# A fused attention, state-space and expert layer on one core: three reorderings (lone late matmuls ahead of the turns, the time step's additions between context differences, a projection over all columns)

## The chip, the cores and the metric

The kernel runs on one core of a Trainium2 chip. The metric is the device time of one execution in microseconds (us), the median of several runs. TensorE multiplies matrices and writes to PSUM, VectorE (DVE in the profile), ScalarE (ACT) and GpSimd (POOL) work on elements, SyncE (SP) issues most transfers. PEld is TensorE's loading of weights.

## What is computed

A layer of a perceiver for a batch of 16 sequences of 128 rows and 512 channels, in 32 bit floating point throughout. Cut to what matters:

```python
x = x + xattn(layernorm(x), ctx)        # 16 heads of 32; 2048 context rows a sequence
x = x + mamba_block(layernorm(x))       # below, then rmsnorm, an MLP of 2048, rmsnorm
x = x + experts(layernorm(x))           # a shared and an expert product, a gate of 7

# in mamba_block, inner width 1024, state 16:
x, z  = split(Z @ in_proj)
x     = silu(causal_conv(x))
dt, B, C = split(x @ x_proj, [32, 48])  # 32 + 16 + 16 columns
dt    = softplus(dt @ dt_proj + b)
h[t]  = exp(dt*A) * h[t-1] + dt * B * x
y     = (sum over states of h*C + x*D) * silu(z)
return y @ out_proj
```

## The kernel before

The program is written in an order set out by hand: each engine executes its instructions in the order in which the Python code issues them, and semaphores keep the data right between the engines.

The attention is cut into 256 steps, `u` = 0 to 255 (L1196): 16 sequences, 4 blocks of 512 context rows for each, 4 groups of 4 heads for each block. After these, 58 more steps and a rest finish the state-space scans and the MLP. In a step the following stands in this order:

- `scores(u)` (L297): four products of queries and keys into four PSUM banks (bank 0 to 3), and `weighted(u - 1)` (L341), the values of the step before under its weights.
- `maxima` (L307, VectorE) and `exps` (L314, ScalarE) read each bank.
- `x_products` (L274) and, at the step's end, `y_products` (L286) make the keys and values of the next block. They are a seven-product scheme for 2 x 2 blocks (the table at L189): the products take blocks of the context, or differences of them, t1 to t4, which GpSimd forms in `ctx_sums` (L221) at steps with u % 4 == 1. The first `y_products` after that need t2, the `x_products` of the next step need t3.
- `turn(u, i, bank)` (L329), i = 0 to 3: four transposes of the weights into a bank, which ScalarE copies out (VectorE for i = 2).
- In between, on VectorE, ScalarE and GpSimd, a quarter of the scan of one chunk of 128 channels: `decays` (L659, exponentials of dt), `inputs` (L637, dx times B), `scan` (L674, twice a step).

Other work is put into the steps by dictionaries of due steps (L1079 to L1136): `late` for matmuls after the turns, `behind` for those after them, `middle`, `inner`, `after`, `head` and `loads` for the rest. Those that matter here:

- `scaled(b, 0)` (L456) at u % 16 == 3: transposes of the shares `fx` into a bank, which VectorE multiplies with `avs`. `turned(b)` (L386) at u % 16 == 10: transposes of the normed x, which VectorE copies out (L391). In some steps with u % 16 == 10 other late matmuls stand beside it.
- A late matmul gets bank 3, 0, 1, ... in turn (`places`, L1257), or the bank of `avp` or `pc` in some steps. If it takes one of the four banks, only three turns are done before it, and the fourth goes behind it, into the next bank (L1263 to L1279). With a single late matmul in bank 3 the fourth turn goes into bank 0.
- `dt_first`, `dt_second`, `dt_third` (L607, L622, L629) make the time step of a chunk. `dt_third` is two additions and a product of 128 x 256 on GpSimd (L631, L632, L634): dt, which `decays` reads, and dx, which `inputs` reads. It is due in `inner`, at the end of steps with u % 4 == 0, from u = 52 on, every fourth step, 64 times.
- `x_proj(g)` (L577), once for each of 8 pairs of sequences, is a product with 64 columns of weights (32 + 16 + 16) in eight parts, each part two instructions on TensorE. Its weights lie in `xproj`, 8 x 64 columns a partition.

Of the kernel before, what the change touches and what calls it, by code (L numbers as in the profile page):

```python
# [8 lines left out]
FP = mybir.dt.float32  # L9
# [6 lines left out]
P = 128  # L16
# [4 lines left out]
DI, DS, DTR = 1024, 16, 32  # L21
EC = DI // P
# [3 lines left out]
GT = GB * NQ  # L26
# [8 lines left out]
def perceiver_layer(ctx: ExitStack, tc: tile.TileContext, a: dict, out: bass.AP):  # L35
    nc = tc.nc
# [21 lines left out]
    bcd = [dram.tile([2 * DS, GT], FP, tag=f"bcd{g}", name=f"bcd{g}") for g in range(B // GB)]  # L58
# [50 lines left out]
    with ExitStack() as es:  # L109
        acon = es.enter_context(tc.tile_pool(name="acon", bufs=1))  # L110
# [7 lines left out]
        def acon_in(name, shape, src=None):  # L118
            t = acon.tile(shape, FP, tag=name, name=name)
            nc.gpsimd.dma_start(t, a[name] if src is None else src)  # L120
            return t
# [3 lines left out]
        banks = [psum.tile([P, 512], FP, tag=f"s{j}", name=f"bank{j}") for j in range(4)]  # L125
# [95 lines left out]
        def ctx_sums(g, names):  # L221
            b11, b12, b21, b22 = (ctx_t[g, j, c] for j in range(2) for c in range(2))
            for n in names:
                t = pool.tile([P, 2, 256], FP, tag=n, name=f"{n}_{g}", bufs=1)
                cfac[g, n] = t
                x, y = {
                    "t1": lambda: (b12, b11),
                    "t2": lambda: (b22, cfac[g, "t1"]),
                    "t3": lambda: (b22, b12),
                    "t4": lambda: (b21, cfac[g, "t2"]),  # L230
                }[n]()
                nc.gpsimd.tensor_tensor(t, x, y, ALU.subtract)  # L232
# [247 lines left out]
            moments_of(b)  # L480


        xproj = acon_in("xproj", [P, EC, DTR + 2 * DS])
        convw = acon_in("convw", [P, EC, 4])
        convb = acon_in("convb", [P, EC])
        dtb = acon_in("dtb", [P, EC])
# [3 lines left out]
        zTs, xas, zss, bcs, dts, wts, ysum, wts_in = ({} for _ in range(8))  # L490
# [84 lines left out]
            sgs.clear()  # L575

        def x_proj(g, ps):  # L577
            ps = ps[0 : DTR + 2 * DS, 0:GT]
            for ec in range(EC):
                nc.tensor.matmul(  # L580
                    ps, xproj[:, ec, :], xas[g, ec], start=(ec == 0), stop=(ec == EC - 1)
                )
            nc.vector.tensor_copy(xd[0 : DTR + 2 * DS, :], ps)
            nc.sync.dma_start(bcd[g], xd[DTR : DTR + 2 * DS, :])

        def load_bc(t, base):

# [11 lines left out]
        xd = ssm.tile([P, GT], FP, tag="xd", name="xd", bufs=1)  # L599
# [29 lines left out]
        def dt_third(g, ec):  # L629
            dt, e, u = dts[g, ec]  # L630
            nc.gpsimd.tensor_tensor(dt, dt, e, ALU.subtract)  # L631
            nc.gpsimd.tensor_tensor(dt, dt, u, ALU.add)  # L632
            dx = ssm.tile([P, GT], FP, tag="dx", name="dx")
            nc.gpsimd.tensor_tensor(dx, dt, xas[g, ec], ALU.mult)  # L634
            dts[g, ec] = dt, dx
# [118 lines left out]
        def flat(ps):  # L754
            return ps.rearrange("p k q -> p (k q)")
# [320 lines left out]
            )  # L1076


        late, after, inner, middle, loads, head, behind = ({} for _ in range(7))  # L1079

        def put(where, u, f):
            where.setdefault(u, []).append(f)

        for b in range(B):
            s = 16 * b
# [21 lines left out]
        for g in range(NG):  # L1107
            p = 32 * (g + 1)
            for ec in range(EC):
                put(loads, p + 8 + ec, lambda g=g, ec=ec: load_win(g, ec))  # L1110
                put(loads, p + 8 + ec, lambda g=g, ec=ec: load_win(g, EC + ec))
                put(late, p + 9 + ec, lambda ps, g=g, ec=ec: x_part(g, ec, ps))
                put(late, p + 9 + ec, lambda ps, g=g, ec=ec: z_part(g, ec, ps))
                put(after, p + 10 + ec, lambda g=g, ec=ec: silu_first(g, ec, xas))
                put(after, p + Z_GATES[ec], lambda g=g, ec=ec: silu_first(g, ec, zss))
            put(late, p + 18, lambda ps, g=g: x_proj(g, ps))
            s = p + LAG
            for ec in range(EC):
                put(loads, s - 4 + 4 * ec, lambda ec=ec: load_dtproj(ec))
                put(behind, s - 3 + 4 * ec, lambda ps, g=g, ec=ec: dt_first(g, ec, ps))  # L1120
                put(middle, s - 2 + 4 * ec, lambda g=g, ec=ec: dt_second(g, ec))
                put(inner, s - 2 + 4 * ec, lambda g=g, ec=ec: dt_third(g, ec))
            for i in range(GB):
                for ec in range(WS):
                    put(loads, s + 32 + 2 * i, lambda g=g, i=i, ec=ec: load_wout(g, i, ec))
                put(loads, s + 31 + 2 * i, lambda b=g * GB + i: reload_x(b))
                put(late, s + 33 + 2 * i, lambda ps, g=g, i=i: projected(g, i, ps))
# [68 lines left out]
        for u in range(last):  # L1196
            live = u < NU
            g, r = divmod(u - 32 - LAG, 32)
            scans = 0 <= g < NG

            made, phase = divmod(u + 3, 4)
            makes = 0 < made < B * SB
            of, phase = ("k", "v")[phase // 2], phase % 2
            load_bc(u + 2 - 32 - LAG, 0)
            if u % 4 == 1 and made + 1 < B * SB:
                load_ctx(made + 1, ("c00", "c10", "c11"))
            if u % 4 == 2 and made + 1 < B * SB:
                load_ctx(made + 1, ("c01",))
            for f in loads.get(u, ()):
                f()  # L1210
            if scans:
                decays(g, r, 0)
            if u > NU:
                while fed < feeds * (u - NU) // (last - 1 - NU):
                    feed(fed)
                    fed += 1
            load_bc(u + 1 - 32 - LAG, DS)
            if u == NU + 1:
                load_rows()
            if live:  # L1220
                scores(u)
            if 1 <= u <= NU:
                weighted(u - 1)
            if u == NU:
                att.close()
                give_back(flat(pa), banks[2], banks[1], flat(avp))
                open_ffn()
            if u == NU + 8:
                load_wex()
            for f in head.get(u, ()):  # L1230
                f()
            if live:
                maxima(u)
            if makes:
                x_products(of, made, phase, pa, pc)
            if live:
                exps(u)
            if makes and u % 4 == 1:
                ctx_sums(made, ("t1", "t2"))
            if 0 <= u + 1 - 32 - LAG < 32 * NG:  # L1240
                inputs(*divmod(u + 1 - 32 - LAG, 32))
            if makes and u % 4 == 1:
                ctx_sums(made, ("t3", "t4"))
            silu_third()
            if scans:
                scan(g, r, 0)
            if makes:
                hold(of, made, pa, "u1")
            if scans:
                decays(g, r, 1)  # L1250
            if makes:
                x_sums(of, made, phase, pa, pc)

            after_turns = late.get(u, ())
            places = [banks[(3 + i) % 4] for i in range(len(after_turns))]  # L1257
            if live and after_turns:
                if u % 4 == 0:
                    places = [flat(avp), *places[:-1]]  # L1260
                elif u % 2 and makes and u not in behind:
                    places[-1] = flat(pc)
            taken = sum(any(p is b for b in banks) for p in places)  # L1263
            if live:
                for i in range(3 if taken else 4):
                    turn(u, i, i)
            if scans:
                scan(g, r, 1)
            for f in middle.get(u, ()):
                f()  # L1270
            for f, ps in zip(after_turns, places):
                if live:
                    f(ps)
                else:
                    ps = bank()
                    f(ps)
                    give_back(ps)
            if live and taken:
                turn(u, 3, (3 + taken) % 4)  # L1279
            for f in behind.get(u, ()):  # L1280
                ps = flat(pc) if makes else banks[2] if live else bank()
                f(ps)
                if not live:
                    give_back(ps)
            for f in after.get(u, ()):
                f()
            for f in inner.get(u, ()):
                f()
            if makes:
                y_products(of, made, phase, pa, pc)  # L1290
                y_sums(of, made, phase, pa, pc)
            silu_second()
# [76 lines left out]
```

## Time and profile before

| | us |
|---|---|
| median of 3 runs | 3802.73 (3801.78 to 3805.72) |
| the profiled execution's own time | 3809.03 |
| its span, first to last instruction | 3807.2 |
| TensorE busy in the span | 3747.0 |
| from 44 to 3110 us, the attention's steps: TensorE busy of 3066.0 | 3044.5 |
| from 3110 us on: TensorE busy of 697.0 | 666.6 |

The mean granted clock of TensorE is 0.993 of full speed. The steps of the attention take 9.2 us (three block products) to 18.0 us (four, with a late projection in it).

How to read it: a row of a timeline gives start, duration, engine, line of the kernel, operation, what it writes and reads (out<-in), the shape, and xN for N instructions run together; in square brackets the idle time before it and what ended it. The ends of matmuls are modelled, and they overlap the next start, so times between starts are the surer measure on TensorE.

### The profile page before, as it was taken

How to read it: one execution, taken by the hardware profiler on the slowest of the kernel's cores; microseconds unless marked ns; L12 is line 12 of the kernel's file. 1: busy time of each engine (PE TensorE's matmuls, PEld its weight loads, DVE VectorE, ACT ScalarE, POOL GpSimd, SP SyncE). 2: the span in 40 equal slices, each digit the busy share in tenths (PEclk: the TensorE clock that was granted, in tenths of full speed). 3: DMA queues.
4: the chain of work that ended last, by engine and by line, in shares of the span. 5: the costliest groups of instructions: out<-in, count | busy, mean ns of one | idle time of the engine just before them, and what ended most of it. 6: DMA issues, size and time to landing. Idle time of an engine off the chain costs nothing.

```text
span 3807.2 us, 70317 instructions
## 1 busy us (share of the span) xinstructions
PE 3747.0 (98%) x26120; PEld 2858.7 (75%) x26120; DVE 2690.4 (71%) x4852; ACT 2443.9 (64%) x5847; POOL 2107.1 (55%) x1968
## 2 busy tenths in 40 slices
PE   8999999999999999999999999999999989999999
PEld 7878787778777877787778878787878766655555
DVE  3444445887878777877787778877887777767843
ACT  3555556777767776777677767776777665545421
POOL 2111213675667665766676566666676667567730
PEclk9999999999999999999999999999999989999999
DMA  3111122444444435353534353445344457577752
GB/s 101 34 40 43 55 65 79 136 154 139 137 162 141 156 120 176 129 166 118 175 131 156 116 187 128 148 134 178 131 148 136 159 186 263 191 256 257 263 194 72
DMA packets 341223, 548.40 MB, mean 144 GB/s; under 512 B 24432, under 2 KB 225408, under 8 KB 340624
## 3 DMA queue, kind: packets, MB, share of 16 engines
q1 hardware_dynamic: 340464, 543.28, 43.2%
q8 instruction: 206, 3.38, 0.4%
q14 instruction: 137, 1.12, 0.1%
q0 software_dynamic: 416, 0.63, 0.1%
HBM read 527.29 MB, written 16.52 MB: 143 GB/s over the span
## 4 chain that ended last, share of the span: by engine, by line
PE 90%; DVE 5%; ACT 3%; issue 1%; POOL 1%; DMA 1%; SPq 0%; DVEq 0%; POOLq 0%; ACTq 0%
PE pa L240 24%; PE pc L240 17%; PE bank L333 11%; PE bank L302 7%; PE avp L346 6%; PE bank L526 4%; PE bank L873 3%; PE bank L968 2%; PE bank L842 2%; PE bank L472 2%; PE avp L399 1%; PE bank L707 1%; PE pc L707 1%; PE pa L873 1%; PE pc L526 1%
## 5 line engine op out<-in xcount | busy, mean ns | idle before, releaser
L310 DVE TENSOR_REDUCE nm<-bank 128x1 f32<-128x512 f32 x1024 | 635.3, 682 | 250.2 <-PE bank L302 250.0
L694 POOL TENSOR_TENSOR ysum<-ysum,w 128x512 f32<-128x512 f32 x384 | 500.7, 1304 | 487.7 <-DVE hst L657 305.8
L320 ACT ACTIVATE pr<-bank,nm 128x512 f32<-128x512 f32 x1024 | 689.8, 687 | 101.0 <-DVE nm L310 97.0
L643 POOL TENSOR_TENSOR w<-dx,bc 128x512 f32<-128x512 f32 x512 | 653.0, 1296 | 4.7
L678 DVE TENSOR_TENSOR_SCAN hst<-hst,w 128x512 f32<-128x512 f32 x456 | 557.0, 1221 | 12.8 <-ACT hst L664 8.5
L338 ACT COPY pT<-bank 128x512 f32<-128x512 f32 x816 | 434.9, 585 | 183.2 <-PE bank L333 179.4
L333 PE MATMUL bank<-ident,pr 128*128 128x128 f32 x4096 | 517.5, 274 | 14.4 <-ACT pr L320 10.5
L664 ACT ACTIVATE hst<-dt,alog 128x254 f32<-128x254 f32 x912 | 436.5, 479 | 145.5 <-DVE hst L657 126.1
L333 PEld LDWEIGHTS bank<-ident,pr 128*128 128x128 f32 x4096 | 471.4, 142 | 66.1 <-ACT pr L320 17.0
L346 PEld LDWEIGHTS avp<-pT,v 128*32 128x32 f32 x8192 | 208.6, 110 | 195.0 <-issue 177.4
L681 DVE TENSOR_TENSOR w<-hst,bc 128x512 f32<-128x512 f32 x456 | 315.2, 691 | 21.2 <-DMA bc<-bcd 5.7
L232 POOL TENSOR_TENSOR t<-c,c 128x512 f32<-128x512 f32 x128 | 164.4, 1285 | 259.4 <-PE pc L240 253.2
L302 PE MATMUL bank<-kt,qT 32*128 32x512 f32 x2048 | 301.3, 643 | 0.9 <-ACT pT L338 0.9
L346 PE MATMUL avp<-pT,v 128*32 128x128 f32 x8192 | 277.6, 276 | 0.0
L240 PE MATMUL pa<-t,ks 128*128 128x256 f32 x1024 | 249.8, 387 | 6.1 <-POOL t L232 6.1
L240 PE MATMUL pa<-vs,t 128*128 128x256 f32 x1008 | 244.7, 386 | 0.0
L240 PEld LDWEIGHTS pa<-t,ks 128*128 128x128 f32 x1024 | 184.8, 190 | 44.2 <-issue 10.6
L240 PEld LDWEIGHTS pa<-vs,t 128*128 128x128 f32 x1008 | 185.4, 190 | 34.6 <-issue 10.1
L320 ACT ACTIVATION_READ_ACCUMULATOR pr<-bank,nm 128x1 f32 x1024 | 209.9, 205 | 0.0
L336 DVE COPY pT<-bank 128x512 f32<-128x512 f32 x208 | 143.8, 691 | 89.6 <-PE bank L333 88.1
L232 POOL TENSOR_TENSOR t<-c,t 128x512 f32<-128x512 f32 x128 | 163.4, 1276 | 36.5 <-issue 19.6
L526 PE MATMUL bank<-zT,win 128*128 128x256 f32 x792 | 182.7, 381 | 0.0
(319 smaller groups left out, 6890.4 us busy)
## 6 DMA issues: line engine op xcount, KB each, us to landing
bc<-bcd SPq DMA_DIRECT2D x512, 512.0 KB, 4.3
c<-in_ctxT_dram SPq DMA_DIRECT2D x256, 256.0 KB, 4.3
wf<-in_w_dram SPq DMA_DIRECT2D x128, 512.0 KB, 7.0
wqo<-in_wqkvo_dram SPq DMA_DIRECT2D x128, 256.0 KB, 4.9
win<-in_win_dram SPq DMA_DIRECT2D x128, 256.0 KB, 4.5
wout<-in_wout_dram SPq DMA_DIRECT2D x128, 256.0 KB, 4.0
x<-in_x_dram SPq DMA_DIRECT2D x16, 256.0 KB, 4.3
x1d<-x SPq DMA_DIRECT2D x16, 256.0 KB, 2.1
```

Of the source, the lines that this page charges most:

```text
L240: nc.tensor.matmul(ps[:, r, :], l[:, kc, r * P : (r + 1) * P], m[:, kc, :], start=(i in (1, 2, 5) and r == 0 and kc == 0), stop=(r == 1 an ...
L302: nc.tensor.matmul(banks[j], qts[b][rows, hg, :], kts[u // 4, hg][rows, :], start=True, stop=True)
L310: nc.vector.tensor_reduce(stats[b][0][j][:, sb, hg : hg + 1], banks[j], AX.X, ALU.max, negate=True)
L320: nc.scalar.activation(pr[:, j, :], banks[j], AF.Exp, bias=nm[j][:, sb, hg : hg + 1], accum_out=sm[:, sb, h : h + 1],)
L333: nc.tensor.transpose(ps[:, j, :], prs[u][:, j, i * P : (i + 1) * P], ident)
L338: nc.scalar.copy(pT, ps)
L346: nc.tensor.matmul(avp[j * HD : (j + 1) * HD, hg, :], vts[u // 4, hg // 2, i // 2][:, i % 2, hg % 2 * P + j * HD : hg % 2 * P + (j + 1) * HD],
L526: nc.tensor.matmul(ps, w[:, kc, :], zTs[g][:, kc, :], start=(kc == 0), stop=(kc == KC - 1))
L643: nc.gpsimd.tensor_tensor(w, dx.unsqueeze(1).to_broadcast([P, NH // 2, GT]), bcs[g * 32 + r, 0][:, i * NH // 2 : (i + 1) * NH // 2, :], AL ...
L664: nc.scalar.activation(bt(h[:, k, :])[:, :, 1:], bt(dt)[:, :, 1:], AF.Exp, scale=aneg[:, ec, n : n + 1],)
L678: nc.vector.tensor_tensor_scan(flat, flat, w.rearrange("p n t -> p (n t)"), 0.0, ALU.mult, ALU.add)
L694: nc.gpsimd.tensor_tensor(s, s, w, ALU.add)
```

## The change

Three edits, independent of each other.

1. `xproj` gets 64 more columns, set to zero by a memset on VectorE at the start; `x_proj` takes 128 columns of weights for each part (its own 64 and the next part's) and writes all 128 partitions of the bank. VectorE still copies the first 64 rows.
2. `dt_third` moves from the end of a step with u % 4 == 0 to the next step, between the differences t1, t2 and `inputs`; t3 and t4 follow `inputs` as before.
3. In a step with u % 16 of 3 or 10 and exactly one late matmul, this is issued ahead of the turns, into bank 3, and all four turns follow in banks 0 to 3. That is so for `scaled(b, 0)` at u = 19, 35, ..., 243 (fifteen steps) and for `turned` at u = 10, 26, 58, 90, 122, 154, 186, 218. VectorE's read of that bank is then also issued ahead of its copy of turn 2 and of the second `scan`.

```diff
-        xproj = acon_in("xproj", [P, EC, DTR + 2 * DS])
+
+        NX = DTR + 2 * DS
+        xproj = acon.tile([P, EC * NX + P - NX], FP, tag="xproj", name="xproj")
+        nc.gpsimd.dma_start(xproj[:, 0 : EC * NX], a["xproj"].rearrange("p a b -> p (a b)"))
+        nc.vector.memset(xproj[:, EC * NX :], 0.0)
...
         def x_proj(g, ps):
-            ps = ps[0 : DTR + 2 * DS, 0:GT]
+            ps = ps[:, 0:GT]
             for ec in range(EC):
                 nc.tensor.matmul(
-                    ps, xproj[:, ec, :], xas[g, ec], start=(ec == 0), stop=(ec == EC - 1)
-                )
-            nc.vector.tensor_copy(xd[0 : DTR + 2 * DS, :], ps)
-            nc.sync.dma_start(bcd[g], xd[DTR : DTR + 2 * DS, :])
+                    ps,
+                    xproj[:, ec * NX : ec * NX + P],
+                    xas[g, ec],
+                    start=(ec == 0),
+                    stop=(ec == EC - 1),
+                )
+            nc.vector.tensor_copy(xd[0:NX, :], ps[0:NX, :])
+            nc.sync.dma_start(bcd[g], xd[DTR:NX, :])
...
-                put(inner, s - 2 + 4 * ec, lambda g=g, ec=ec: dt_third(g, ec))
+                put(between, s - 1 + 4 * ec, lambda g=g, ec=ec: dt_third(g, ec))
...
             if makes and u % 4 == 1:
                 ctx_sums(made, ("t1", "t2"))
+            for f in between.get(u, ()):
+                f()
             if 0 <= u + 1 - 32 - LAG < 32 * NG:
                 inputs(*divmod(u + 1 - 32 - LAG, 32))
...
+
+            ahead = live and u % 16 in (3, 10) and len(after_turns) == 1
+            if ahead:
+                after_turns[0](banks[3])
+                after_turns, places = (), ()
             taken = sum(any(p is b for b in banks) for p in places)
```

More of the change, by code (lines that the diff above doesn't have):

```diff
@@ L1076, in perceiver_layer @@
             )
-        late, after, inner, middle, loads, head, behind = ({} for _ in range(7))
+        late, after, inner, middle, loads, head, behind, between = ({} for _ in range(8))
         def put(where, u, f):
```

## The prediction

> **What bounds the kernel now.** I read the page first, then who waits for whom on TensorE, then the timelines of TensorE, GpSimd and VectorE in the steps that the change touches.
>
> ```profile
> PE 3747.0 (98%) x26120; PEld 2858.7 (75%) x26120; DVE 2690.4 (71%) x4852; ACT 2443.9 (64%) x5847; POOL 2107.1 (55%) x1968
> PE 90%; DVE 5%; ACT 3%; issue 1%; POOL 1%; DMA 1%; SPq 0%; DVEq 0%; POOLq 0%; ACTq 0%
> ```
>
> TensorE is busy 98% of the span and is 90% of the chain that ended last. A gain can only come from TensorE having less to do or waiting less. Its waits:
>
> ```profile
> PE pa L240 <- POOL t L232: 6.1, 12, 0.5
> ...
> PE bank L333 <- ACT pT L338: 3.3, 6, 1.3
> ```
>
> The columns are total us, times, longest. Twelve waits for a context difference and six for a copy out of a bank: these two rows are what the change can reach. "Idle" there counts from modelled ends of matmuls, so I work below with starts. In an undisturbed stream a transpose starts 0.109 us after the one before, a 256-column product 0.216 us.
>
> **Part 1: the time step's additions behind the first two differences.** At u % 16 == 5, from u = 69 to 245, twelve times, TensorE looks like this (u = 165):
>
> ```profile
> 1993.98 1.91 PE L333 MATMUL bank<-ident,pr 128*128 128x128 f32 x16
> 1996.39 1.99 PE L240 MATMUL pa<-t,ks 128*128 128x256 f32 x8 [0.50 <-POOL t L232]
> ...
> 2000.40 1.99 PE L240 MATMUL pa<-t,ks 128*128 128x256 f32 x8
> ```
>
> Sixteen transposes from 1993.98 end their issue at 1993.98 + 16 x 0.109 = 1995.72; the next product starts at 1996.39, so 0.67 us is lost. It needs t2. GpSimd in that stretch:
>
> ```profile
> 1985.94 1.46 POOL L694 TENSOR_TENSOR ysum<-ysum,w 128x512 f32<-128x512 f32 x1 [3.37 <-DVE hst L657]
> 1987.35 4.11 POOL L467 TENSOR_TENSOR aT<-aT,avs 128x512 f32<-128x512 f32 x3
> 1991.42 0.72 POOL L631 TENSOR_TENSOR dt<-dt,e 128x256 f32<-128x256 f32 x1
> 1992.22 0.72 POOL L632 TENSOR_TENSOR dt<-dt,l 128x256 f32<-128x256 f32 x1
> 1993.02 0.73 POOL L634 TENSOR_TENSOR dx<-dt,xa 128x256 f32<-128x256 f32 x1
> 1993.71 1.27 POOL L232 TENSOR_TENSOR t<-c,c 128x512 f32<-128x512 f32 x1
> 1995.06 1.28 POOL L232 TENSOR_TENSOR t<-c,t 128x512 f32<-128x512 f32 x1
> 1996.29 2.50 POOL L643 TENSOR_TENSOR w<-dx,bc 128x512 f32<-128x512 f32 x2
> 1998.74 1.28 POOL L232 TENSOR_TENSOR t<-c,c 128x512 f32<-128x512 f32 x1
> ```
>
> From 1985.94 GpSimd never rests. The change puts the three additions (2.33 us) behind t1 and t2. These then end at 1991.42 + 1.27 + 0.08 + 1.27 = 1994.04, which is 1.7 us before TensorE asks. The wait of 0.67 us goes.
>
> What is late next is t3, the last row shown. The order after is t1, t2, dt, dt, dx, w, w, t3: the same work, started from the same release by VectorE, which hangs on the step before and does not move. So t3 ends no earlier than now, 2000.02. It ends slightly later: the rows show 0.08 us between an operation and one that reads its result, against an overlap of 0.04 otherwise. Now one such gap (t1 to t2) and two (L631, L632, L634) are there; after, w follows dx at once and reads it, a gap in place of an overlap: 0.12 us more, t3 at 2000.14. Add 0.055 us from t2's end (1996.34) to its product (1996.39): TensorE can start on t3 at 2000.20. It starts now at 2000.40 and would arrive at 2000.40 - 0.67 = 1999.73. So 0.47 us of the 0.67 comes back as a wait for t3 in the next step, and 0.20 remains: 12 x 0.20 = 2.4 us. In the other steps with these additions t2 is ready 1.8 us or more before its product, and t3 2.1 us or more, so nothing is gained or lost there.
>
> What the move delays: dt by two differences, 2.55 us. Its first reader is the exponential at L664 on ScalarE. In the attention's steps that starts at least 5.9 us after dt is done (1992.94 and 1998.90 here), so 2.7 us are left once TensorE comes 0.67 us earlier: no cost. Behind the attention there are no differences, and the additions stay directly ahead of w, except twice, where two additions of b2 (L883, 2.5 us) now go first. In the first of these ScalarE already waits 2.0 us for dt and would wait 2.5 longer (3468.10 to 3470.6); in the other about 1.1 (3540.69 to 3541.8). VectorE uses these decays only at 3475.53 and 3548.79, and ScalarE's next operations lie at 3473.82 and 3547.07: hidden. Without that cover it would be 3.6 us in all, which I keep for the range.
>
> **Part 2: a lone late matmul ahead of the turns.** Two kinds. At u % 16 == 10, where `turned` is alone (u = 10, 26, 58, 90, 122, 154, 186, 218), TensorE at u = 154 shows:
>
> ```profile
> 1874.21 1.47 PE L333 MATMUL bank<-ident,pr 128*128 128x128 f32 x12
> 1875.52 0.60 PE L389 MATMUL bank<-ident,xn 128*128 128x128 f32 x4
> 1876.53 0.66 PE L333 MATMUL bank<-ident,pr 128*128 128x128 f32 x4 [0.41 <-ACT pT L338]
> ```
>
> The fourth turn uses bank 0 and waits for ScalarE's copy of the first: 1876.53 - (1875.52 + 4 x 0.109) = 0.57 us. After, `turned` starts at 1874.21, the turns at 1874.65, and the fourth turn, on bank 3, is due at 1874.65 + 12 x 0.109 = 1875.96. It must wait for VectorE's copy of bank 3 (L391), now issued ahead of the second scan, right behind these sums:
>
> ```profile
> 1874.48 0.88 DVE L260 SCALAR_TENSOR_TENSOR kt<-pc,bk,u1k 128x256 f32<-128x256 f32 x2
> ```
>
> They end at 1875.36; the copy starts 0.08 us before that end, as neighbours in this row do, takes 0.69, and 0.06 us later the turn may start: 1876.03. A wait of 0.07 takes the place of 0.57: 0.50 us gained, five times (u = 90 to 218), 2.5 us. At u = 58 ScalarE's exponentials are late; `turned` on bank 3 must then sit out the last of them, and the sums end at 695.01, so the fourth turn starts at 695.67 in place of 696.19: 0.5 us. At u = 10 and 26 there is no wait now, and the new one costs 0.07 each. Sum: 2.5 + 0.5 - 0.1 = 2.9 us.
>
> At u % 16 == 3 `scaled` is alone (u = 19 to 243, fifteen times), and no wait is seen there now. After, VectorE's product (L464, 0.68) follows one sum (L270, 1971.54 to 1972.23 at u = 163): 1972.23 - 0.08 + 0.68 + 0.06 = 1972.89, and the fourth turn is due at 1971.27 + 0.44 + 1.31 = 1973.02. Nothing gained, 0.12 us short of a loss. Behind the matmul on TensorE all four turns are queued, but its inputs are there over 3 us earlier and bank 3 is free when the last exponential ends, which the first turn needs too. The read-out passes VectorE's copy of turn 2 and a scan; these come up to 0.7 us later, and VectorE idled 0.41 us before the next maxima here.
>
> **Part 3: x_proj over 128 columns.** The row first (u = 50):
>
> ```profile
> 601.15 1.47 PE L333 MATMUL bank<-ident,pr 128*128 128x128 f32 x12
> 602.55 3.67 PE L580 MATMUL bank<-xa,xproj 128*64 128x256 f32 x16
> 606.15 0.65 PE L333 MATMUL bank<-ident,pr 128*128 128x128 f32 x4
> ```
>
> 12 x 0.109 puts its due start at 602.46, 16 x 0.216 its due end at 606.01; it runs 0.09 late in and 0.09 late out, eight times: 8 x 0.19 = 1.5 us. The Trainium skill, "TensorEngine Tiling (Array Packing)", Key Properties, says that a change of tiling mode drains the engine, and the row fits that: full-width neighbours show no such gap. A rule that speaks against the change is in "TensorE: Matmul & The Clock Gate", LDWEIGHTS: a load's time goes with its columns, columns / 1.2 ns. By it 128 loads grow by 53 ns each, 6.8 us if nothing hid them. The trace has 137 ns for 64 columns and 190 for 128, and products with 128-column loads still start every 0.216 us: the load lies under the product ahead. By the rows 0, and I take 0. The last of the eight lies behind the attention and sits out 3.4 us for GpSimd (xa, L574), which swallows the way in: 1.4 us in all. The new memset stands beside two like it (0.27 and 0.17 us at L601 and L602), where VectorE then idles 2.1 us for its first input: 0. The read-out still takes 64 rows.
>
> **The sum.** 2.4 + 2.9 + 1.4 = 6.7 us. The profiled execution took 3809.0 us (span 3807.2) and would take 3802.3; it lies 6.3 above the median of 3802.7, so the median becomes 3796.0.
>
> **Rivals.**
> - All of part 1 is kept: t3 is no bar, because GpSimd's string starts earlier or the product asks later. 12 x 0.67 = 8.0, with 4.3 from the rest 12.3 us: 3790.4. Against it: the string has no idle time, and the 0.38 us between t3 and its product is in every one of the twelve. 0.18.
> - Part 1 is worth nothing, or the tail's 3.6 us is not hidden: only about 3 us remain, 3799.7. The idle ScalarE speaks against it. 0.17.
> - Slower: VectorE reads bank 3 out later than reckoned, say behind one more operation of 0.69 us, because its sums come late. The place is the fourth turn in all 23 steps: 15 x (0.69 - 0.12) + 8 x 0.69 = 14 us lost against 6.7 gained: 3810. It decides from a delay of about 0.35 us. For it: the margin is only 0.12 us. Against: VectorE idled 0.26 us before L270. 0.08.
> - The forecast: 3796.0, own range 3793.5 to 3798.5. 0.57.
>
> About 0.2% (7.6 us) is what a measurement of this kernel can tell from no change. Below 3795.1 lies the first rival and a third of the forecast: 0.37. Slower by that: 0.06. The rest: 0.57. The range, 3790.0 to 3800.5, takes in the first two rivals.
>
> **What would show it.** In the profile after: no wait of L240's t2 at u % 16 == 5, and in the next step a wait for t3 with about 0.47 us late; at u % 16 == 10 a fourth turn 0.07 us late on VectorE's copy; none at u % 16 == 3; x_proj rows of 128*128 with no gap at either end. I am wrong if t3 does not appear among TensorE's waits, if fourth turns wait 0.3 us or more, or if the stretch behind the attention changes its length by over 2 us.

## The result, and the profile after

| | before | after |
|---|---|---|
| median, us (8 runs each, on one chip) | 3806.18 (3801.78 to 3807.61) | 3796.10 (3789.46 to 3799.43) |
| profiled execution: own time | 3809.03 | 3798.45 |
| profiled execution: span | 3807.2 | 3796.7 |
| start of step 8 to start of step 250 | 2927.3 | 2916.1 |

The ratio is 0.9969 (95% interval 0.9959 to 0.9978): 8 to 16 us faster, 0.3%. The time forecast, 3796.0, and the time measured, 3796.1, are closer than they deserve to be. The gain forecast was 6.7 us, from a median of 3 runs; with 8 runs the median of before lies 3.5 us higher, and the gain lies below the interval. What was missed is found below.

The last row of the table is the surest measure here. It runs from the first product of `scores` (L302) in step 8 to that in step 250, read off the trace. Nearly all steps that an edit does not touch repeat to 0.02 us from one profile to another (the largest stray difference is 0.09), while what lies before and behind the steps does not: in the nine profiles of this study step 8 starts at 118.1 to 123.1 us, and the stretch from the last step's start on takes 699.6 to 706.6 us.

The page after (two of its rows), and who TensorE waits for:

```profile
PE 3737.2 (98%) x26120; PEld 2861.7 (75%) x26120; DVE 2701.5 (71%) x4853; ACT 2446.3 (64%) x5847; POOL 2108.8 (56%) x1968
...
PE 86%; DVE 5%; POOL 3%; ACT 2%; issue 2%; DMA 2%; SPq 0%; POOLq 0%; DVEq 0%; ACTq 0%
```

```profile
PE pa L240 <- POOL t L232: 6.2, 12, 0.5
...
PE bank L333 <- DVE xnT L391: 0.5, 1, 0.5
```

TensorE has lost 10 us of busy time with the same number of instructions. Yet the row of waits for a context difference is nearly the same as before, 12 waits and 6.2 us (6.1 before): they have moved, not gone. In the chain GpSimd has gone from 1% to 3%. The row of waits for ScalarE's copy pT is gone, with one wait for VectorE's copy xnT (at u = 58) in its place.

By length of step, after against before, summed over steps with a difference of over 0.03 us:

| steps | which | sum, us |
|---|---|---|
| u % 16 == 10 | five of -0.52, u = 58 -0.42; u = 10 and 26 +0.11 each | -2.80 |
| u % 16 == 5 | twelve of about -0.77 | -9.29 |
| u % 16 == 6 | twelve of about +0.58 | +7.00 |
| u % 16 == 4 | twelve of -0.39 | -4.68 |
| u % 32 == 18, x_proj | seven of -0.29 | -2.03 |
| u % 32 == 2 | five of about +0.12, one of -0.05 | +0.54 |

They come to -11.3 us; the steps lost 11.2. The span lost only 10.5: the stretches before and behind the steps are 0.7 us longer together, within what differs from run to run.

**The additions.** Step 165 and the start of 166 on TensorE, to be held against the first timeline of before:

```profile
1986.39 1.91 PE L333 MATMUL bank<-ident,pr 128*128 128x128 f32 x16
1988.14 1.89 PE L240 MATMUL pa<-t,ks 128*128 128x256 f32 x8
...
1992.62 1.99 PE L240 MATMUL pa<-t,ks 128*128 128x256 f32 x8 [0.51 <-POOL t L232]
```

The product with t2 follows the transposes at once (1986.39 + 16 x 0.109 = 1988.13), and the next step's product with t3 now has the wait. GpSimd in the same stretch:

```profile
1978.36 1.46 POOL L702 TENSOR_TENSOR ysum<-ysum,w 128x512 f32<-128x512 f32 x1 [2.63 <-DVE hst L665]
...
1983.84 1.27 POOL L232 TENSOR_TENSOR t<-c,c 128x512 f32<-128x512 f32 x1
1985.18 1.27 POOL L232 TENSOR_TENSOR t<-c,t 128x512 f32<-128x512 f32 x1
...
1988.84 2.50 POOL L651 TENSOR_TENSOR w<-dx,bc 128x512 f32<-128x512 f32 x2
1991.29 1.28 POOL L232 TENSOR_TENSOR t<-c,c 128x512 f32<-128x512 f32 x1
```

From the string's start to t3's end it took 2000.02 - 1985.94 = 14.08 us before; now 1992.57 - 1978.36 = 14.21: 0.13 more, where 0.12 was reckoned. TensorE starts 0.05 after t3.

**The lone matmul at u % 16 == 10** (u = 154, TensorE):

```profile
1867.41 0.60 PE L389 MATMUL bank<-ident,xn 128*128 128x128 f32 x4
1867.85 2.02 PE L333 MATMUL bank<-ident,pr 128*128 128x128 f32 x16
1869.70 1.89 PE L240 MATMUL pc<-c,ks 128*128 128x256 f32 x8
```

Sixteen turns take 1869.70 - 1867.85 = 1.85 us, where 16 x 0.109 is 1.74: 0.11 is still lost. Half of it is the wait: the first transpose of the fourth turn starts at 1869.21, due at 1869.16. The other half comes after it: the next transpose starts 0.165 us later in place of 0.109. Before, the wait of 0.57 had the same 0.06 behind it, so that 0.63 has become 0.11.

**x_proj** (u = 178):

```profile
2155.48 3.62 PE L584 MATMUL bank<-xa,xproj 128*128 128x256 f32 x16
2158.94 0.60 PE L333 MATMUL bank<-ident,pr 128*128 128x128 f32 x4
2159.37 1.89 PE L240 MATMUL pc<-c,ks 128*128 128x256 f32 x8
```

From its start to the turn's it is 3.46 us (16 x 0.216) where it was 3.60 (in u = 50 and u = 178 alike), and the turn behind it takes 0.43 where it took 0.49.

### The profile page after: what moved, and what is told of

It reads as the page before. It is cut to its first block, busy times and chain, and to the rows that moved or that the text cites. A ratio compares the mean times of both kernels' runs of the same rounds, so it can differ in the third digit from the quotient of the medians.

```text
span 3796.7 us, 70358 instructions
## 1 busy us (share of the span) xinstructions
PE 3737.2 (98%) x26120; PEld 2861.7 (75%) x26120; DVE 2701.5 (71%) x4853; ACT 2446.3 (64%) x5847; POOL 2108.8 (56%) x1968
## 4 chain that ended last, share of the span: by engine, by line
PE 86%; DVE 5%; POOL 3%; ACT 2%; issue 2%; DMA 2%; SPq 0%; POOLq 0%; DVEq 0%; ACTq 0%
PE pa L240 22%; PE pc L240 16%; PE bank L333 11%; PE bank L302 6%; PE avp L346 6%; PE bank L530 4%; PE bank L881 3%; PE bank L976 2%; PE bank L850 2%; PE bank L472 2%; PE avp L399 1%; PE bank L715 1%; POOL t L232 1%; PE pc L715 1%; ACT pr L320 1%
## 5 line engine op out<-in xcount | busy, mean ns | idle before, releaser
L346 PEld LDWEIGHTS avp<-pT,v 128*32 128x32 f32 x8192 | 208.6, 110 | 195.1 <-issue 177.6
L302 PE MATMUL bank<-kt,qT 32*128 32x512 f32 x2048 | 296.8, 643 | 0.0
L346 PE MATMUL avp<-pT,v 128*32 128x128 f32 x8192 | 277.6, 276 | 0.0
```

The lines of the kernel that those rows point to most:

```text
L302: nc.tensor.matmul(banks[j], qts[b][rows, hg, :], kts[u // 4, hg][rows, :], start=True, stop=True)
L346: nc.tensor.matmul(avp[j * HD : (j + 1) * HD, hg, :], vts[u // 4, hg // 2, i // 2][:, i % 2, hg % 2 * P + j * HD : hg % 2 * P + (j + 1) * HD],
```

## The experiments

Each kernel is the one before or after with the edit shown. Lengths are for step 8 to step 250; before 2927.3, after 2916.1.

### The projection alone

The two hunks of the diff for `xproj` and `x_proj`, put on the kernel before.

> The kernel before with the 128-column projection alone. If the gaps at both ends of the projection come from its 64 columns: each of the seven steps with x_proj in the attention is 0.29 us shorter, 2.0 us in all, loads at about 190 ns hidden under products that start every 0.216 us; no other step changes. If the wider loads cost time on TensorE (53 ns each): those steps get 0.6 us longer in place of shorter. Whole kernel: about 2 us faster, below what the timing resolves.

Measured: ratio 0.9987 (0.9981 to 0.9994); steps 2925.5. The seven steps are 0.29 us shorter each, 2.03 in all, and no other step differs by more than 0.03. Loads take 190 ns (137 before) and are hidden. The gain is that of the width alone.

### The additions alone

```diff
-                put(inner, s - 2 + 4 * ec, lambda g=g, ec=ec: dt_third(g, ec))
+                put(between, s - 1 + 4 * ec, lambda g=g, ec=ec: dt_third(g, ec))
...
+            for f in between.get(u, ()):
+                f()
```

> The kernel before with the move of the time step's additions alone. Theory: steps u % 16 == 5 get 0.77 us shorter (9.3 us in the twelve), steps u % 16 == 6 get 0.58 longer by the wait for t3 (7.0 us), and the steps with u % 32 == 2 from 98 on get 0.12 longer, because VectorE's L440 waits for GpSimd's string, which ends 0.12 later; net 1.7 us faster. Rival, that t3's lateness needs the other parts of the change: 9 us faster with no longer step 6.

Measured: ratio 0.9996 (0.9988 to 1.0005), not to be told from no change; steps 2925.8, 1.5 shorter. Steps u % 16 == 5: -9.29; u % 16 == 6: +6.97; u % 32 == 2: six of about +0.12, 0.72 in all; u = 58: +0.12. So the wait for t3 is this part's own doing, and the rival falls.

### The lone matmul ahead at u % 16 == 3 alone

```diff
+            ahead = live and u % 16 in (3,) and len(after_turns) == 1
+            if ahead:
+                after_turns[0](banks[3])
+                after_turns, places = (), ()
```

> The kernel before with the lone matmul ahead of the turns at u % 16 == 3 alone. Theory: the step with u % 16 == 3 keeps its length, and the next one gets 0.39 us shorter twelve times, 4.7 us in all, because its fourth scores product no longer waits for VectorE's late read of bank 3. Rival, that the additions' move shortened steps u % 16 == 4: nothing changes here.

Measured: ratio 0.9988 (0.9981 to 0.9994); steps 2922.7. Twelve steps with u % 16 == 4, from 68 to 244, are 0.39 us shorter, 4.68 in all, and no other step differs by more than 0.03. The additions have no part in it.

### The lone matmul ahead at u % 16 == 10 alone

The same with `(10,)`.

> The kernel before with the lone matmul ahead of the turns at u % 16 == 10 alone. Theory: five steps 0.52 us shorter, u = 58 0.42 shorter, u = 10 and 26 0.11 longer: 2.8 us faster. No other step changes.

Measured: ratio 0.9993 (0.9984 to 1.0002); steps 2924.7. Five of about -0.52, u = 58 -0.51, two of +0.11, and u = 66 -0.05: -2.93 in all. In the kernel after, u = 58 gains only 0.42, as the additions alone make it 0.12 longer. The sums of the four parts, each put alone on the kernel before, are 2.03, 1.48, 4.68 and 2.93 us (the lone matmul counted by its two places): 11.1 of the 11.3 found in the kernel after.

### VectorE's read ahead, TensorE's order kept

```diff
+            early = live and u % 16 == 3 and len(after_turns) == 1
+            if early:
+                after_turns[0](places[0])
+                after_turns = ()
             if scans:
                 scan(g, r, 1)
```

It stands behind the first turns, so TensorE's order in these steps is that of before; only VectorE's read comes ahead of the scan.

> The kernel before, where at u % 16 == 3 TensorE keeps its order (three turns, the lone matmul, the fourth turn in bank 0 or, at u = 19 and 35, the matmul in the other bank behind all turns), and only VectorE's read of that matmul is issued ahead of the second scan. If the 0.39 us in the next step are the fourth scores product waiting for that late read: the same twelve steps get 0.39 us shorter, 4.7 us in all. If it is the order on TensorE, or bank 0 against bank 3 for the fourth turn: no change.

Measured: ratio 0.9986 (0.9977 to 0.9996); steps 2923.0. The same twelve steps, 0.39 each, 4.68 in all, as with the matmul ahead; two others are 0.09 (u = 82) and 0.04 longer, for a reason that was not found. Two rows of before show where it was lost. Step 164's scores on TensorE, and VectorE's read of bank 3 from step 163:

```profile
1975.70 1.53 PE L302 MATMUL bank<-kt,qT 32*128 32x512 f32 x8
```

```profile
1975.38 0.68 DVE L464 TENSOR_TENSOR aT<-avs,bank 128x512 f32<-128x512 f32 x1
```

The four products of `scores` go to banks 0 to 3. The read ends at 1976.06, 0.36 us after they start, and the row takes 1.53 us where step 165's takes 1.14. Within the row, the first three of the four products start at 1975.70 to 1975.72, and the fourth at 1976.11, 0.05 us after the read's end. In step 165 all four start within 0.02 us. In this experiment VectorE's read and TensorE's row are:

```profile
1967.85 0.68 DVE L464 TENSOR_TENSOR aT<-avs,bank 128x512 f32<-128x512 f32 x1
```

```profile
1970.17 1.14 PE L302 MATMUL bank<-kt,qT 32*128 32x512 f32 x8
```

The read ends 1.64 us before the scores start, and the 0.39 is gone. So the gain is that of the early read. The matmul's place ahead of the turns is one way to get it.

### t3 also ahead of the additions

```diff
-                ctx_sums(made, ("t1", "t2"))
+                ctx_sums(made, ("t1", "t2", "t3") if u in between else ("t1", "t2"))
...
-                ctx_sums(made, ("t3", "t4"))
+                ctx_sums(made, ("t4",) if u in between else ("t3", "t4"))
```

> The kernel after, with t3 also ahead of the time step's additions in the steps that have them (t1, t2, t3, additions, inputs, t4). If what came back is the wait for t3: the twelve steps with u % 16 == 6 get 0.58 us shorter, 7.0 us in all against the kernel after, and about 18 us against the kernel before (0.9953). dt then comes 1.3 us later still, with an estimated 1.5 us left before ScalarE asks. If something else than t3 holds TensorE back there, they keep their length. The 0.12 us at u % 32 == 2 stay, as GpSimd's string keeps its extra gap.

Measured: median 3785.34, ratio to before 0.9943 (0.9930 to 0.9955); steps 2909.2. The twelve steps u % 16 == 6 are 7.00 us shorter than in the kernel after, each as long as before the change, and the gain at u % 16 == 5 stays. TensorE's waits for a context difference have no row left. In steps 165 and 166 both products now follow at once, as t3 ends at 1983.48, over 4 us before the second one starts:

```profile
1982.20 1.28 POOL L232 TENSOR_TENSOR t<-c,c 128x512 f32<-128x512 f32 x1
```

```profile
1983.92 1.89 PE L240 MATMUL pa<-t,ks 128*128 128x256 f32 x8
...
1987.82 1.99 PE L240 MATMUL pa<-t,ks 128*128 128x256 f32 x8
```

The 0.12 us at u % 32 == 2 stay (0.13 to 0.14), as expected. This kernel is faster than both.

### t3 between the additions and inputs

```diff
             for f in between.get(u, ()):
                 f()
+            if makes and u % 4 == 1 and u in between:
+                ctx_sums(made, ("t3",))
```

with `t4` alone behind `inputs` in these steps.

> The kernel after, with t3 between the additions and inputs (t1, t2, additions, t3, inputs, t4). t3 is then done before TensorE asks, as in the run with t3 ahead of the additions: 7.0 us shorter than the kernel after in the steps u % 16 == 6. Besides, w no longer follows dx at once, so GpSimd's string loses the 0.12 us again; if VectorE's L440 waits for the end of that string, the 0.12 us at u % 32 == 2 (five steps against the kernel before) go too, 0.6 us. If L440 waits for something else, they stay.

Measured: median 3787.05, ratio to before 0.9947 (0.9935 to 0.9960); steps 2908.5, the shortest. The steps u % 16 == 6 are again 7.00 shorter than after, and the five with u % 32 == 2 are 0.49 shorter together, so that four of them are as before. The intervals of the last two kernels overlap: which is faster, the times do not tell.

The medians of these two kernels lie 22.2 and 20.5 us below that of before, and the steps account for 18.1 and 18.8. The rest lies mostly behind the steps: from the last step's start on it takes 701.8 and 702.9 us, against 705.6 before. The code there is that of the kernel after, which took 706.6, so the edits are not the reason. The profile shows a granted clock of 1.00 in 135 us of that stretch (3291 to 3426) in the kernel with t3 ahead, and of 0.96 in the same part of the kernel after; why it differs is not shown.

The 0.12 us at u % 32 == 2 come in through an operation that has no data in common with GpSimd's string. In step 161 VectorE's L440, 128 x 64 numbers, takes this in the kernel before, against GpSimd's t4:

```profile
1954.32 1.12 DVE L440 TENSOR_TENSOR sm<-sm,nm 128x64 f32<-128x64 f32 x1
```

```profile
1954.09 1.27 POOL L232 TENSOR_TENSOR t<-c,t 128x512 f32<-128x512 f32 x1
```

And in the kernel after:

```profile
1947.00 1.24 DVE L440 TENSOR_TENSOR sm<-sm,nm 128x64 f32<-128x64 f32 x1
```

```profile
1946.89 1.27 POOL L232 TENSOR_TENSOR t<-c,t 128x512 f32<-128x512 f32 x1
```

Where GpSimd is idle (u = 17) it takes 0.22 us. Here it ends 0.08 us behind t4 in both kernels (1955.44 behind 1955.36, 1948.24 behind 1948.16). There are sixteen of these operations in a profile; in 11 to 13 of them a GpSimd operation has over 0.1 us still to run when L440 starts, and L440 then ends 0.08 or 0.09 us behind it (once 0.12). VectorE works without a pause from there to the sums of step 162 (L260), which free `pc`, for which TensorE then waits 0.07 us. The Trainium skill, "SBUF — State Buffer", Who interferes with whom, states that a VectorE instruction with two SBUF inputs contends with a GpSimd instruction that reads SBUF, as its second input comes through the shared read interface. The rows agree. So does VectorE's product L681, which reads one input from PSUM (`hst`, L127): in the kernel before it takes 0.69 us in the 152 cases in which GpSimd works beside it for over 90% of the time and in the 219 in which GpSimd is idle. And taking the 0.12 us out of GpSimd's string took nearly all of it out of TensorE's step.

## Why the prediction was right or wrong

- **The additions, 2.4 us.** Right in kind and size for what was reckoned: 0.77 gained and 0.58 given back a step leave 0.19, against 0.20. Both are about 0.1 larger than put (0.67 and 0.47), and for one reason. A wait for t2 cost 0.1 beyond itself: before, the second product of that group starts 0.32 us after the first instead of 0.216. Without the wait that goes too, TensorE comes 0.1 earlier to t3, and waits 0.1 longer for it, so the 0.20 that remains is not touched. Not reckoned was L440. GpSimd's 0.12 us were put into the sum for t3 alone; they cost 0.54 elsewhere (and 0.1 at u = 58), so the part brought 1.7, and 1.5 by itself.
- **The lone matmul at u % 16 == 10, 2.9 us.** Right: 2.8. The new wait is 0.05, put at 0.07. What a wait costs in the transposes behind it, 0.06, was left out; it falls away between two waits, as at u = 154, and is why u = 10 and 26 lost 0.11 in place of 0.07.
- **The lone matmul at u % 16 == 3, "Nothing gained, 0.12 us short of a loss".** Wrong, and this is the step that failed: 4.7 us gained. The working followed the matmul to the end of its own step, where indeed nothing changed, and asked whether the new order makes a fourth turn wait. It did not ask who else waits for the late read of bank 3. VectorE's read ended at 1976.06, and the next step writes bank 3 at 1975.7. No list of waits shows it: the idle time is reckoned from modelled ends, and the four score products overlap, so the wait sits inside a busy row. Its length, 1.53 against 1.14, was there to be read, as were the late start of the fourth product within it and step 164's 12.63 us against 12.2 at u = 20.
- **x_proj, 1.4 us.** Right in its mechanism, too small in size: 0.29 a step in place of 0.19. The way out was written down as 0.09 although the rows gave 0.14 (606.15 against 606.01), and the turn behind it was 0.06 slower, which was not looked at. The rule that wider loads cost time would have made these steps longer; they are shorter, and the loads are hidden.
- **The memset, dt's later landing, the stretch behind the attention.** Nothing measurable. No step of the attention waits for dt. Behind the attention ScalarE's longest wait for dt has grown from 2.0 to 4.4 us, close to the 2.5 more that were forecast, and from the last step's start on it takes 706.6 us against 705.6, inside the spread from run to run.

The likeliest case of the prediction, part of the additions' gain given back to t3, is what happened, but the whole gain is over 0.2%, which had a chance of 0.37, because of the early read.

## What to carry to other kernels

When a result leaves a bank, a buffer or a port earlier, ask for every later user of it, in the next step too: the wait may sit inside a row that counts as busy, and a row longer than its equals is the sign of it. When a wait for one result of an engine's string is removed by reordering, the next result of the same string is the next wait; here moving it too brought 7.0 us, where the reordering had brought 1.7. In a schedule whose steps repeat to hundredths of a microsecond, the lengths of single steps show gains of 1.5 and 2.9 us (the additions, the lone matmul at u % 16 == 10) for which the interval of the whole time includes no change.

## What the runs showed of the hardware

In the groups shown, a 256-column product on TensorE that comes after a wait is followed by its neighbour 0.1 us later than in a stream (0.32 against 0.216). The same 0.1 stands, with no wait, in the first group behind the 32-column products of L346 (1.99 us for eight products in place of 1.89). A transpose after a wait is followed 0.06 us later than in a stream (0.165 against 0.109), and so is the first full-width transpose behind the 64-column products. VectorE's small operation with two inputs in SBUF (0.22 us by itself) took up to 1.25 us beside a GpSimd operation, and ended 0.08 us behind it; a larger one with one input in PSUM took 0.69 us with and without GpSimd beside it.
